# The shared expert's last 64 channels computed by token beside the router and carried in the expert rows

## The chip, the cores and the metric

The kernel runs on one NeuronCore of one Trainium2 chip. The time is that of one execution on the device in microseconds, as a median over runs. A core has five engines that matter here, each with its own queue of instructions: TensorE (PE in the profile; its weight loads are PEld), VectorE (DVE), ScalarE (ACT), GpSimd (POOL) and SyncE (SP), which here issues most of the DMA transfers.

## The reference

Everything is float32. 2048 tokens of 256 channels go through a layer norm, an attention-like block (convolution, gates, a scan over time, a perceptron), another norm and a residual, and then through a mixture of experts. The change is in the last part:

```python
shared = silu(x @ sw_gate) * (x @ sw_up) @ sw_down        # 704 inner channels
logits = x @ router_w.T                                   # 8 experts
top_w, top_i = top_k(softmax(logits), 2);  top_w /= sum(top_w)
h = silu(einsum('th,ehi->eti', x, w_gate)) * einsum('th,ehi->eti', x, w_up)   # 176 inner channels
expert_out = einsum('eti,eih->eth', h, w_down)
routed = einsum('eth,te->th', expert_out, combine)        # combine: the two weights, which sum to 1
out = routed + sigmoid(x @ shared_gate_w)[:, None] * shared
x = x + layernorm(out)
```

The shared expert has 704 = 5 x 128 + 64 inner channels, so in chunks of 128 there are five whole ones and a tail of 64. A routed expert has 176 = 128 + 48.

## The kernel before, in words

The tokens are worked in 8 blocks of 256 (`TB`), each seen as two halves of 128 (`NT`). A matrix product over 256 channels is two accumulating TensorE products (`product`, line 385), and each shows in the profile as two records.

*The three stages.* From 0 to about 360 us the attention, the perceptron, the routing and, for blocks 0 to 3, the shared expert are interleaved: every part of a block is a generator or a list of named steps, each step has a place (one unit is one of the perceptron's eight chunks), and all steps are sorted by place (`places`, `runs`). `runs` gives `route` of a block 8 places and `shared` nine evenly spaced ones (`evenly(NS + 4)`, with NS = 5). Within that order the compiler's scheduler may still move an instruction that is ready ahead of one that is not; each engine then executes its own list in order. `behind(...)` pins the order on the named engines where it is used. Then, from about 398 to 488 us, the routed experts are worked in 36 blocks of 128 rows (`in_turn`, `routed`), four steps deep: while block i is being transposed, i-1 does its gate and up products, i-2 its second transposes and i-3 its down product. At the end (`closing`, a list written out by hand) the shared expert of blocks 5 to 7 is interleaved with fetching, combining, normalizing and storing. Block 4's shared expert (`kept`) and the first three chunks of block 5's fill TensorE at the turn from the first stage to the second.

*`route(b)`* (lines 755 to 835). Normalizes the tokens into `ln` with `W` = 259 values to a row (256 channels, the first pair number, the chosen expert, the weight), transposes them to `yT` (channels on partitions), multiplies by `w_r` (9 columns: 8 logits and the shared gate), copies the logits to `lg` on VectorE, finds the two best, makes the weight and the gate on ScalarE (a tanh) and GpSimd, counts ranks with two small products, and scatters each token's row twice into the DRAM table `xs` by four indirect DMAs from GpSimd's queue, sorted by expert. `ln` has two buffers.

*`shared(b)`* (lines 840 to 877). For each of five chunks: gate and up products from `yT` into one PSUM bank, silu on ScalarE, product on VectorE into `shid`. Sixth step: one chunk that holds 64 up and 64 gate channels, so half as many products. Then for each half of the tokens a down product over six chunks of `shid` and `s_down`, of which the sixth is padded with zero rows, and the gate is applied by ScalarE (blocks 0 to 4) or VectorE (blocks 5 to 7, line 872).

*The turn.* `tables` works out from the counts where each expert's rows start and which expert each of the blocks of 128 rows belongs to; `fill` writes zero rows behind each expert's last one (eight DMAs on SP's queue, line 935). A branch (`tc.If`, for a few extra blocks) follows.

*`routed(i)`* (lines 937 to 986). SP reloads 128 rows into `xb` (4 buffers), after all scatters; TensorE transposes them, VectorE copies to `xT` and works out `pair` and `share` from the row's last three values; TensorE multiplies by the expert's gate and up weights (352 columns); silu and product go into one of two halves of `padded`, 256 wide with zeros behind the 176; two transposes, a copy on ScalarE (`hT`), and a down product of two steps, where the second has 48 weight rows and zeros. ScalarE scales by `share` (minus the weight for the first choice, one minus it for the second), and GpSimd's queue scatters the result into `ys`. VectorE's queue has `pair` of a block ahead of the copy to `xT` of an earlier one. `pair` has eight buffers, freed as the scatter of its block has ended.

*The closing.* `fetch` reads both rows of each token back (`g`), `combine` adds them (line 999 to 1002), `finish` normalizes and stores; `finish_last` does so for each half of block 7.

PSUM has eight banks: two "A", one "B", three "M", one "S", one "D". `route` takes "M", and so does the perceptron.

Of the kernel before, what the change touches and what calls it, by code (L numbers as in the profile page):

```python
# [9 lines left out]
F32 = mybir.dt.float32  # L10
# [9 lines left out]
P = 128  # L20
# [7 lines left out]
def kernel(ctx: ExitStack, tc: tile.TileContext, a: dict, out: bass.AP):  # L28
# [21 lines left out]
    assert T % TB == 0 and NT == 2 and KC == 2 and P < I <= 2 * P and TAIL == 64 and E == 8  # L50
# [34 lines left out]
    W = C + 3  # L85
    zeros = const.tile([P, W], F32, name="zeros")
    nc.gpsimd.memset(zeros, 0.0)
    nc.gpsimd.memset(zeros[:, C : C + 1], float(T * TOPK))
# [32 lines left out]
    def in_rows(ap):  # L121
        return ap.rearrange("(k p) n -> p k n", p=P)
# [82 lines left out]
    s_gu = wpool.tile([P, KC, (2 * NS + 1) * P], F32, name="s_gu")  # L205
# [7 lines left out]

    s_down = wpool.tile([P, NS + 1, C], F32, name="s_down")
    nc.sync.dma_start(s_down[:, 0:NS, :], in_rows(a["sw_down"][0 : NS * P, :]))
    nc.sync.dma_start(s_down[0:TAIL, NS, :], a["sw_down"][NS * P :, :])
# [4 lines left out]
    w_r = const.tile([P, KC, E + 1], F32, name="w_r")  # L221
# [69 lines left out]
    def tables_ready():  # L291

        to_columns((r_rows, w_r))
        nc.vector.tensor_copy(count, count_i)
        nc.vector.tensor_scalar(first_rows, experts_iota, float(ES), None, ALU.mult)
        nc.vector.tensor_scalar(block_rows, count, float(P), None, ALU.mult)
        nc.gpsimd.tensor_copy(first_pair, first_pair_i)
        nc.gpsimd.memset(seen, 0.0)
        nc.gpsimd.memset(s_down[TAIL:, NS, :], 0.0)
        nc.gpsimd.memset(shid[TAIL:, NS, :], 0.0)  # L300
# [91 lines left out]
    shid = act.tile([P, NS + 1, TB], F32, name="shid")  # L392
# [342 lines left out]
    KEEP_FROM, LATE_FROM, AHEAD, OFTEN = 4, 5, 3, 36  # L735
# [18 lines left out]
    def route(b):  # L754
# [5 lines left out]
        normalize("R", ln[:, :, 0:C], x_tiles[b], mv, rs)  # L760
        nc.gpsimd.tensor_copy(ln[:, :, C], first_pair[:, b * NT : (b + 1) * NT])
        yield
        yT = act.tile([P, KC, TB], F32, tag="yT", name=f"yT_{b}", bufs=NB - KEEP_FROM + 1)
        nc.scalar.copy(yT, to_channels("M", ln))
        yield
        po = psum("M")
        for n in range(NT):
            product(
                po[:, n * 16 : n * 16 + E + 1],
                [yT[:, k, tok(n)] for k in range(KC)], [w_r[:, k, :] for k in range(KC)],  # L770
            )
        lg = small.tile([P, NT, E + 1], F32, tag="lg", name=f"lg_{b}")
        nc.vector.tensor_copy(
            lg, po[:, 0 : NT * 16].rearrange("p (n e) -> p n e", n=NT)[:, :, 0 : E + 1]
        )
# [13 lines left out]
        nc.gpsimd.tensor_scalar(ln[:, :, C + 2], th[:, :, 0], 0.5, 0.5, ALU.mult, ALU.add)  # L789
        nc.gpsimd.tensor_scalar(gate, th[:, :, 1], 0.5, 0.5, ALU.mult, ALU.add)  # L790
        idf = small.tile([P, NT, TOPK], F32, tag="idf", name=f"idf_{b}")
        nc.vector.tensor_copy(idf, idx[:, :, 0:TOPK])
        nc.gpsimd.tensor_copy(ln[:, :, C + 1], idf[:, :, 0])
# [46 lines left out]
    def shared(b, banks=cycle("S"), shid=shid):  # L840

        t = live[b]
# [4 lines left out]
        for f in range(NS + 1):  # L847
            po = psum(next(banks))
            if f < NS:
                product(po[:, 0:TB], chunk(f), rhs)  # L850
                product(po[:, TB:], chunk(NS + f), rhs)
                nc.scalar.activation(shid[:, f, :], po[:, 0:TB], AF.Silu)
                nc.vector.tensor_tensor(shid[:, f, :], shid[:, f, :], po[:, TB:], ALU.mult)  # L853
            else:
                product(po[:, 0:TB], chunk(2 * NS), rhs)
                nc.scalar.activation(shid[0:TAIL, f, :], po[TAIL:, 0:TB], AF.Silu)
                nc.vector.tensor_tensor(  # L857
                    shid[0:TAIL, f, :], shid[0:TAIL, f, :], po[0:TAIL, 0:TB], ALU.mult
                )
            yield  # L860
        f_ = part_of[b] if b >= LATE_FROM else new_part(b)
        for n in range(NT):
            pn = psum(next(banks))[:, 0:C]
            product(
                pn, [shid[:, f, tok(n)] for f in range(NS + 1)],
                [s_down[:, f, :] for f in range(NS + 1)],
# [70 lines left out]
    def routed(i, row_i, off_i, of):  # L937
# [3 lines left out]
        xb = moe.tile([P, W], F32, tag="xb", name=f"xb_{i}", bufs=4)  # L941
        after(nc.sync.dma_start(xb, xs[bass.ds(at, P), :]).ins, scatters)
        pt = psum("A")
        for k in range(KC):
            nc.tensor.transpose(pt[:, tok(k)], xb[:, tok(k)], ident)  # L945
# [4 lines left out]
            pair, xb[:, C + 1 : C + 2], of[:, i : i + 1], xb[:, C : C + 1], ALU.not_equal, ALU.add  # L950
# [4 lines left out]
            share, xb[:, C + 1 : C + 2], of[:, i : i + 1], xb[:, C + 2 : C + 3], ALU.not_equal,  # L955
            ALU.subtract,
# [8 lines left out]
        h = padded[:, i % 2, :]  # L965
# [67 lines left out]
    def evenly(n):  # L1033
# [15 lines left out]
        (shared, NB, evenly(NS + 4)),  # L1049
# [47 lines left out]
    def keep():  # L1097
        nonlocal kept, shids
        more = wpool.tile([P, NS + 1, TB], F32, tag="w_gate", name="shid2")
        nc.gpsimd.memset(more[TAIL:, NS, :], 0.0)  # L1100
        shids = cycle((more, shid))
        kept = shared(KEEP_FROM, all_banks, next(shids))
        next(kept)
# [6 lines left out]
    for place, _, run in steps:  # L1110
        if place >= (NB + 2) * NF and not closed:
# [20 lines left out]
            )  # L1132
        run()
# [4 lines left out]
    padded = moe.tile([P, 2, C], F32, name="padded")  # L1138
    nc.gpsimd.memset(padded[:, :, I:], 0.0)
# [21 lines left out]
    for b in range(LATE_FROM, NB):  # L1161
# [10 lines left out]
        5.3 5.4 5.5 6.0 6.1 C5 C0 5.6 A0 5.7 C1  # L1172
        6.2 A5 N0 6.3 A1 6.4 X0 N5 C2 6.5 N1 C6 7.0 X5 A2 7.1 X1 C3 6.6 N2 A3 6.7 X2 A6 C4
        7.2 A4 N3 7.3 X3 N6 C7 7.4 N4 7.5 X6 X4 7.6 L0 7.7 L1
# [40 lines left out]
```

## Time and profile before

| | |
|---|---|
| median of 3 runs | 542.26 us (542.12 to 542.28) |
| the profiled execution | 542.94 us, its span 541.1 us |
| TensorE busy | 519.6 us, 96%, 2532 records |
| VectorE, ScalarE, GpSimd busy | 331.8, 218.4 and 165.0 us |
| granted TensorE clock | 0.993 |
| router products | 64 records of 128x9 |
| shared expert, gate and up | 352 records of 128x256 |
| shared expert, down | 192 records of 128x256 |
| reloads of rows | 36 of 129.5 KB |

A profile's line for an instruction gives its start in us from the span's start, its length in us, the engine, the line of the kernel, the operation, output and inputs, and behind "x" how many of them were merged. In brackets stands how long the engine had been idle before it and what ended that. A line for a stretch gives the stretch, its length, and the busy time of each engine with its number of instructions, then the granted clock, the DMA engines' share and the rate. Matmuls overlap one another, so that their lengths add up to more than the time they take; the distance from one group's start to the next one's is the pace. A line of the chain gives start, length and what the end of the kernel waited for then.

### The profile page before, as it was taken

How to read it: one execution, taken by the hardware profiler on the slowest of the kernel's cores; microseconds unless marked ns; L12 is line 12 of the kernel's file. 1: busy time of each engine (PE TensorE's matmuls, PEld its weight loads, DVE VectorE, ACT ScalarE, POOL GpSimd, SP SyncE). 2: the span in 40 equal slices, each digit the busy share in tenths (PEclk: the TensorE clock that was granted, in tenths of full speed). 3: DMA queues.
4: the chain of work that ended last, by engine and by line, in shares of the span. 5: the costliest groups of instructions: out<-in, count | busy, mean ns of one | idle time of the engine just before them, and what ended most of it. 6: DMA issues, size and time to landing. Idle time of an engine off the chain costs nothing. (4 is left out here: it accounts for less than half of the span.)

```text
span 541.1 us, 8015 instructions
## 1 busy us (share of the span) xinstructions
PE 519.6 (96%) x2532; PEld 433.8 (80%) x2532; DVE 331.8 (61%) x1100; ACT 218.4 (40%) x500; POOL 165.0 (30%) x297
## 2 busy tenths in 40 slices
PE   8999999999999999999999999998999999999992
PEld 5877677888888888888888888887867777777881
DVE  4788998896997987966824223232444444432883
ACT  4655554544644545433313313222124444442340
POOL 7233202203442432414105204023304334342351
PEclk9999999999999999999999999999999999999997
DMA  4981101001001110110000901001323333314621
GB/s 124 377 250 20 19 2 19 1 1 21 20 21 19 40 18 4 40 21 31 10 1 30 315 15 41 0 2 39 120 80 104 94 99 101 102 56 129 238 79 58
DMA packets 31344, 37.37 MB, mean 69 GB/s; under 512 B 4824, under 2 KB 26180, under 8 KB 31302
## 3 DMA queue, kind: packets, MB, share of 16 engines
q1 hardware_dynamic: 27440, 28.37, 18.6%
q0 software_dynamic: 3584, 8.48, 4.6%
q8 instruction: 21, 0.34, 0.3%
q14 instruction: 21, 0.17, 0.1%
q10 hardware_dynamic: 278, 0.01, 0.0%
HBM read 22.34 MB, written 13.18 MB: 66 GB/s over the span
## 5 line engine op out<-in xcount | busy, mean ns | idle before, releaser
L385 PE MATMUL psM<-h2T,w_gate 128*128 128x256 f32 x256 | 66.4, 381 | 0.0
L385 PE MATMUL psM<-h2T,w_val 128*128 128x256 f32 x256 | 66.1, 379 | 0.0
L710 PE MATMUL psD<-w_out,hid 128*128 128x256 f32 x256 | 63.5, 380 | 0.1
L982 POOL DMA_INDIRECT ys<-yb,pair x36 | 35.4, 983 | 70.6 <-ACT yb L981 59.4
L385 PEld LDWEIGHTS psM<-h2T,w_gate 128*128 128x128 f32 x256 | 47.8, 190 | 8.1 <-DVE o L631 1.3
L710 PEld LDWEIGHTS psD<-w_out,hid 128*128 128x128 f32 x256 | 48.4, 190 | 6.9 <-DVE hid L721 0.5
L385 PEld LDWEIGHTS psM<-h2T,w_val 128*128 128x128 f32 x256 | 48.6, 190 | 6.5
L385 PE MATMUL psM<-m_w,xT 128*128 x144 | 48.9, 462 | 0.7 <-DVE shid L853 0.4
L720 ACT ACTIVATE hid<-psM 128x256 f32<-128x256 f32 x64 | 24.1, 376 | 60.8 <-PE psM L385 60.7
L721 DVE TENSOR_TENSOR hid<-hid,psM 128x256 f32<-128x256 f32 x64 | 26.3, 411 | 31.3 <-ACT hid L720 31.0
L329 POOL TENSOR_SCALAR ln_rs<-ln_mv 128x2 f32<-128x2 f32 (+1 forms) x33 | 8.6, 261 | 117.3 <-DVE ln_mv L321 103.9
L828 POOL DMA_INDIRECT xs<-ln,rows x32 | 32.4, 1011 | 18.6 <-DVE rows L824 8.0
L385 PE MATMUL psA<-yT,s_gu 128*128 128x256 f32 x144 | 34.7, 383 | 2.7 <-DVE shid L853 2.7
L385 PE MATMUL psD<-m_w,hT 128*128 x144 | 37.2, 381 | 0.0
L949 DVE TENSOR_SCALAR pair<-xb,of 128x1 int32<-128x1 f32 x36 | 9.8, 272 | 42.1 <-DMA ys<-yb,pair 33.2
L385 PEld LDWEIGHTS psA<-yT,s_gu 128*128 128x128 f32 x144 | 26.7, 190 | 6.5 <-DVE shid L853 3.3
L385 PEld LDWEIGHTS psM<-m_w,xT 128*128 128x128 f32 x144 | 24.6, 191 | 8.9 <-DVE shid L853 0.6
L385 PEld LDWEIGHTS psD<-m_w,hT 128*128 128x128 f32 x144 | 24.6, 191 | 2.4 <-ACT yb L981 0.5
L330 POOL TENSOR_TENSOR ln_rs<-ln_rs,neg_half 128x2 f32<-128x2 f32 (+1 forms) x33 | 25.3, 766 | 2.2
L981 ACT ACTIVATE yb<-psD,share 128x256 f32<-128x256 f32 x36 | 17.0, 473 | 19.9 <-PE psD L385 16.8
L966 ACT ACTIVATE padded<-psM 128x176 f32<-128x176 f32 x36 | 11.4, 317 | 33.5 <-PE psM L385 27.2
L385 PE MATMUL psA<-s_down,shid 128*128 128x256 f32 x96 | 22.4, 381 | 0.7 <-DVE shid L857 0.7
(266 smaller groups left out, 1073.6 us busy)
## 6 DMA issues: line engine op xcount, KB each, us to landing
xb<-xs SPq DMA_DIRECT2D x36, 129.5 KB
g<-ys SPq DMA_DIRECT2D x8, 512.0 KB
xs<-zeros SPq DMA_DIRECT2D x16, 129.5 KB
x<-in_L_attn_x_dram SPq DMA_DIRECT2D x8, 256.0 KB
decay<-by_head SPq DMA_DIRECT2D x14, 128.0 KB
out_dram<-f SPq DMA_DIRECT2D x7, 256.0 KB
m_w<-in_L_ffn_w_gate_dram SPq DMA_DIRECT2D x2, 704.0 KB
m_w<-in_L_ffn_w_up_dram SPq DMA_DIRECT2D x2, 704.0 KB
```

Source lines behind the costliest of these rows:

```text
L329: nc.gpsimd.tensor_scalar(rs, mv[:, :, 1], EPS, None, ALU.add)
L330: nc.gpsimd.tensor_tensor(rs, rs, neg_half[:, 0:nt], ALU.pow)
L385: nc.tensor.matmul(po, lhs[i], rhs[i], start=(i == 0), stop=(i == len(lhs) - 1))
L710: nc.tensor.matmul(total[:, n * C : (n + 1) * C], hids[f][:, tok(n)], w_out[:, f, :], start=(f == 0 and n == 0), stop=(f == NF - 1 and n = ...
L720: nc.scalar.activation(hid, po[:, 0:TB], AF.Silu)
L721: nc.vector.tensor_tensor(hid, hid, po[:, TB:], ALU.mult)
L828: inst = nc.gpsimd.indirect_dma_start(out=xs, out_offset=bass.IndirectOffsetOnAxis(ap=rows[:, c : c + 1], axis=0), in_=ln[:, n, :], in_off ...
L949: nc.vector.tensor_scalar(pair, xb[:, C + 1 : C + 2], of[:, i : i + 1], xb[:, C : C + 1], ALU.not_equal, ALU.add)
L966: nc.scalar.activation(h[:, 0:I], po[:, 0:I], AF.Silu)
L981: nc.scalar.activation(yb, po[:, 0:C], AF.Copy, scale=share)
L982: inst = nc.gpsimd.indirect_dma_start(out=ys, out_offset=bass.IndirectOffsetOnAxis(ap=pair, axis=0), in_=yb, in_offset=None, bounds_check= ...
```

## The change

The shared expert's tail leaves `shared` and `shid`. Where the router multiplies a token's channels by 9 columns, it now multiplies by 137: 64 up, 64 gate, 8 logits and the gate (`w_r` moves behind them in `s_gu`). ScalarE and VectorE make silu(gate) times up by token (`end`), and GpSimd multiplies it by the shared gate into the token's row. A row of `xs` is now 3 numbers, 256 channels, 64 tail values and 16 zeros, W = 339 values. In `routed` the hidden values are written over the reloaded channels, so that the 176 hidden values, the 64 tail values and the zeros stand side by side, 256 wide, and the second transposes take all of them; `padded` goes, and `xb` has 6 buffers. The second down weights of every expert get the 64 tail rows of `sw_down` below their 48 (one more DMA, 64 rows to each of 8 experts). Each token has two rows and its two weights sum to one, so the tail is added once, and the gate is in it already. `evenly` gets one place fewer, the hand-written closing is arranged anew, and the memsets of the padding rows of `s_down` and `shid` go.

```diff
-    W = C + 3
+    X0 = 3
+    T0 = X0 + C
+    ROW, H0 = T0 + TAIL, T0 - I
+    W = H0 + 2 * P
...
-    s_gu = wpool.tile([P, KC, (2 * NS + 1) * P], F32, name="s_gu")
+    s_gu = wpool.tile([P, KC, (2 * NS + 1) * P + E + 1], F32, name="s_gu")
...
-    s_down = wpool.tile([P, NS + 1, C], F32, name="s_down")
-    nc.sync.dma_start(s_down[:, 0:NS, :], in_rows(a["sw_down"][0 : NS * P, :]))
-    nc.sync.dma_start(s_down[0:TAIL, NS, :], a["sw_down"][NS * P :, :])
+    s_down = wpool.tile([P, NS, C], F32, name="s_down")
+    nc.sync.dma_start(s_down, in_rows(a["sw_down"][0 : NS * P, :]))
...
-    w_r = const.tile([P, KC, E + 1], F32, name="w_r")
+    w_r = s_gu[:, :, (2 * NS + 1) * P :]
...
-        normalize("R", ln[:, :, 0:C], x_tiles[b], mv, rs)
-        nc.gpsimd.tensor_copy(ln[:, :, C], first_pair[:, b * NT : (b + 1) * NT])
+        normalize("R", ln[:, :, X0:T0], x_tiles[b], mv, rs)
+        nc.gpsimd.tensor_copy(ln[:, :, 0], first_pair[:, b * NT : (b + 1) * NT])
+        nc.gpsimd.memset(ln[:, :, ROW:], 0.0)
...
             product(
-                po[:, n * 16 : n * 16 + E + 1],
-                [yT[:, k, tok(n)] for k in range(KC)], [w_r[:, k, :] for k in range(KC)],
-            )
+                po[:, n * C : n * C + P + E + 1],
+                [yT[:, k, tok(n)] for k in range(KC)], [s_gu[:, k, 2 * NS * P :] for k in range(KC)],
+            )
+        by_token = po.rearrange("p (n e) -> p n e", n=NT)
...
+        nc.vector.tensor_copy(lg, by_token[:, :, P : P + E + 1])
+        end = small.tile([P, NT, TAIL], F32, tag="end", name=f"end_{b}", bufs=1)
+        nc.scalar.activation(end, by_token[:, :, TAIL:P], AF.Silu)
+        nc.vector.tensor_tensor(end, end, by_token[:, :, 0:TAIL], ALU.mult)
...
+        nc.gpsimd.tensor_tensor(
+            ln[:, :, T0:ROW], end, gate.unsqueeze(2).to_broadcast([P, NT, TAIL]), ALU.mult
+        )
...
-        for f in range(NS + 1):
+        for f in range(NS):
             po = psum(next(banks))
...
-            else:
-                product(po[:, 0:TB], chunk(2 * NS), rhs)
-                nc.scalar.activation(shid[0:TAIL, f, :], po[TAIL:, 0:TB], AF.Silu)
-                nc.vector.tensor_tensor(
-                    shid[0:TAIL, f, :], shid[0:TAIL, f, :], po[0:TAIL, 0:TB], ALU.mult
-                )
...
-                pn, [shid[:, f, tok(n)] for f in range(NS + 1)],
-                [s_down[:, f, :] for f in range(NS + 1)],
+                pn, [shid[:, f, tok(n)] for f in range(NS)], [s_down[:, f, :] for f in range(NS)],
...
-        xb = moe.tile([P, W], F32, tag="xb", name=f"xb_{i}", bufs=4)
+        xb = moe.tile([P, W], F32, tag="xb", name=f"xb_{i}", bufs=XB)
...
-            nc.tensor.transpose(pt[:, tok(k)], xb[:, tok(k)], ident)
+            nc.tensor.transpose(pt[:, tok(k)], xb[:, X0 + k * P : X0 + (k + 1) * P], ident)
...
-        h = padded[:, i % 2, :]
+        h = xb[:, H0:]
...
-        (shared, NB, evenly(NS + 4)),
+        (shared, NB, evenly(NS + 3)),
...
+            nc.sync.dma_start(
+                m_we[I - P : I - P + TAIL, :, KC * GU + C :],
+                a["sw_down"][NS * P :, :].unsqueeze(1).to_broadcast([TAIL, E, C]),
+            )
...
-        5.3 5.4 5.5 6.0 6.1 C5 C0 5.6 A0 5.7 C1
-        6.2 A5 N0 6.3 A1 6.4 X0 N5 C2 6.5 N1 C6 7.0 X5 A2 7.1 X1 C3 6.6 N2 A3 6.7 X2 A6 C4
-        7.2 A4 N3 7.3 X3 N6 C7 7.4 N4 7.5 X6 X4 7.6 L0 7.7 L1
+        5.3 5.4 6.0 C5 C0 5.5 A0 5.6 C1
+        6.1 A5 N0 6.2 A1 6.3 X0 N5 C2 6.4 N1 C6 7.0 X5 A2 6.5 X1 C3 7.1 N2 6.6 A3 X2 A6 C4
+        7.2 A4 N3 C7 7.3 X3 N6 7.4 N4 X6 7.5 X4 L0 7.6 L1
```

## The prediction

> **What bounds the kernel now.** I read the page's busy lines first, then the stretches of the span, then the costliest TensorE groups, then the order of time.
>
> ```profile
> PE 519.6 (96%) x2532; PEld 433.8 (80%) x2532; DVE 331.8 (61%) x1100; ACT 218.4 (40%) x500; POOL 165.0 (30%) x297
> ```
>
> TensorE is busy 96%, but its matmuls overlap (a 128x256 one lasts 380 ns), so busy is not yet pace. The pace is in the order of time:
>
> ```profile
> 298.50 1.89 PE L385 MATMUL psS<-yT,s_gu 128*128 128x256 f32 x8
> 300.22 1.03 PE L385 MATMUL psM<-h2T,w_gate 128*128 128x256 f32 x4
> ...
> 304.54 0.60 PE L376 MATMUL psM<-ident,ln 128*128 128x128 f32 x4
> 304.98 1.03 PE L385 MATMUL psA<-yT,s_gu 128*128 128x256 f32 x4
> 305.84 1.03 PE L385 MATMUL psM<-h2T,w_gate 128*128 128x256 f32 x4
> ...
> 308.87 0.96 PE L385 MATMUL psM<-w_r,yT 128*128 128x9 f32 x8
> 309.68 2.84 PE L385 MATMUL psS<-s_down,shid 128*128 128x256 f32 x12
> ```
>
> Eight 128x256 records from 298.50 to 300.22: 0.2155 us each. Four 128x128: 0.110 each. Eight 128x9: 0.101 each. (A product in the code is two records: the groups yT,s_gu have 144 + 80 + 64 + 32 + 32 = 352, which is 8 blocks x 22 products x 2.) Counting every form of each stretch with these paces fills 98 to 102% of nearly every 25 us between 100 and 360; TensorE has no holes there. The stretches:
>
> ```profile
> core 0: us, PE busy (x) PEld busy (x) DVE busy (x) ACT busy (x) POOL busy (x), PEclk, DMA share, GB/s
> 100.00:250.00 150.00, 149.93 (x758) 130.09 (x758) 124.69 (x417) 72.39 (x160) 45.84 (x86) 1.00 0.09 18
> 250.00:359.00 109.00, 107.85 (x529) 95.30 (x528) 41.53 (x159) 30.51 (x73) 26.22 (x43) 1.00 0.18 55
> 359.00:398.50 39.50, 37.55 (x184) 32.56 (x184) 15.72 (x71) 9.66 (x24) 11.80 (x16) 1.00 0.21 68
> 398.50:487.60 89.10, 88.38 (x423) 65.45 (x421) 39.03 (x139) 38.95 (x105) 32.44 (x33) 1.00 0.31 91
> 499.70:518.80 19.10, 19.10 (x90) 16.85 (x89) 16.32 (x43) 6.44 (x14) 6.97 (x17) 1.00 0.59 216
> 518.80:534.40 15.60, 11.48 (x52) 9.44 (x51) 11.58 (x30) 4.57 (x10) 6.88 (x15) 0.98 0.22 76
> ```
>
> TensorE sets the pace up to 487; VectorE has room from 250 to 488 (routing and shared stages), but is nearly as full as TensorE in the closing (16.32 of 19.10). The chain says so too: it is all PE to 518.80, then turns to VectorE and GpSimd, and TensorE itself waits there for the tail:
>
> ```profile
> 526.79 0.39 ACT shid L856
> 527.18 0.02 issue
> 527.21 0.41 DVE shid L857
> ```
>
> **The change part by part.** Sums are made against the profiled execution: 542.94 us, its span of 541.1 and 1.84 around it. The median, 542.26, is 0.68 lower, and that is taken off at the end.
>
> *Tail products.* Per block of 256 tokens, two products (gate/up chunk, two k) and one of six in each of two down products go: 4 products, 8 records, 8 x 0.2155 = 1.724 us of TensorE. Eight blocks: 64 records, 13.79 us.
>
> *Router made wider.* The same 64 records grow from 9 to 137 columns. Between 0.110 at 128 and 0.2155 at 256 columns, 137 cost 0.1174; 0.0164 more than now, 1.05 us in all. The weight loads stay as they are. Net TensorE: -12.74 us if nothing else bound.
>
> The page "TensorE: Matmul & The Clock Gate" of the Trainium skill (section "Back-to-back issue gap") gives 262 cycles for 256 columns, at 2.4 GHz 109 ns, and 134 cycles (56 ns) for 128; by it the removal would be worth an estimated 7.0 us, and the gain about half of mine. The rows above show 215 ns and 110 ns for these f32 records, so I go by the rows.
>
> *Up to 359 us.* Tails of blocks 0 to 2 (24 records, 5.17 us) lie here, where the pace is TensorE's alone; seven routers add 0.92. Net -4.25. Each route adds on VectorE one 128x128 product (between the 128x32 row, 188 ns, and the 128x176 one, 336: about 0.30 us) behind a ScalarE silu (between 205 and 317 ns: 0.28), on GpSimd a product by the gate (between 281 ns for 128x2 and 1342 for 128x512: 0.54) and a memset (0.12). VectorE stands in line: the top-two search and whatever of the attention is queued behind wait for that silu. In exchange, later, VectorE loses a 64x256 product (0.41) and ScalarE a silu (0.38) per block. Cover: VectorE idle 25 of 150 us, GpSimd 104. The router's bank of the three "M" ones is held perhaps 0.7 us longer. Bounds: nothing, to 0.2 us per route (1.4); I take 0.3.
>
> *GpSimd beside VectorE.* The 128x2 power took 0.71 at 519.05 and 1.13 at 515.84, while VectorE ran two-input 128x512 operations: here GpSimd was the one that lengthened. "SBUF — State Buffer", section "Who interferes with whom", says that a VectorE instruction with two SBUF inputs and a GpSimd one that reads SBUF exclude each other and the later one blocks; by it VectorE could lose up to an estimated 0.54 us per route, which its idle time still covers.
>
> *Start.* The zero rows are 1356 instead of 1036 bytes (8 x 40 KB more on SP's queue at 30 us, ahead of the decay transfers), one small weight load less. The waits named for the zero rows near there are 0.3 and 0.5 us; bounds 0 to 0.5, taken 0.1. The extra 512 KB of down weights go on SP's queue at some 300 us, where the next on it, the filling at 383, is far off: nothing; without that cover 1.7 us at the 315 GB/s of that slice.
>
> *Turn from shared to routed, 359 to 398.5.* Removed: blocks 3 and 4, 16 records, 3.45 us; one router adds 0.13. But a chain runs through: the last block's router ends at 378.04, the rows are known at 382.5, SP issues fillings from 383.45 to 390.9 and the first reload at 393.21, which lands at 395.19; the first expert transpose is at 398.47, 3.1 us later, because TensorE is still at shared work. There is also a hole of 1.5 us at 371.7. After the change the work between router and first transpose is kept chunks f2 to f4 (5.17), two downs (4.31), small ones (0.6) and three chunks of block 5 (5.17), 15.3 us, against a chain of about 17.1 us (378.04 to 395.19), +0.3 for silu and product, +0.2 for the larger transfer: TensorE waits some 2 us. The router itself ends about where it did (tail and 1.5 us hole less, the second down now ahead of it). So the first transpose comes about 3.0 us earlier (395.5 for 398.5). Bounds 1.5 (the chain 1.5 longer) to 3.8 (all removed work and the 0.45 hole at 392.8).
>
> *Routed blocks.* 36 at 2.49 us, all TensorE (two transposes 0.22, gate/up 1.19, 0.22, down 0.86): the tail rides in rows 48 to 111 of the second down product, which was there already. Same time, unless a wait comes in (rival 2).
>
> *Closing.* Blocks 5 to 7: 24 records, 5.17 us, and the 0.69 that TensorE waits for the tail at 526.98: 5.86 by TensorE. By VectorE: from 499.7 (the first fetch lands) it works some 27 of 34.6 us, loses two products (0.82), and so cannot end sooner than 6 us before now. Neither end is likely to be reached, since both would have to run full; the low bound is what VectorE and the last down lose by themselves, 0.82 + 0.43 + 0.69 = 1.9. I take 4.5, near TensorE's because TensorE leads up to 518.8. What then comes late is the combining and normalizing on VectorE.
>
> Sum: -4.25 + 0.3 + 0.1 - 3.0 - 4.5 = -11.35; 542.94 - 11.35 = 531.6, as a median 530.9. I say 531.0, the likeliest case.
>
> **Rivals.** (1) *The closing is VectorE's.* For it: the chain from 518.8 to 528.8 has no matmul in it, VectorE 85% full before. Against: that stretch is itself late because TensorE brings block 7's first chunk only at 518.6. Then 1.9 of 4.5 are left, perhaps with 1.5 less at the turn: 533.6 to 535.1; 534.3.
>
> (2) *The routed stage gets a wait; slower.* The hidden rows are now written into the reloaded rows' buffer, so a buffer is held until the second transposes, and its reload is released at 1.6 us into a block's period, not at 0.2; six buffers in place of four give back two periods, which the longer hold takes. A reload lands about 2.0 us after issue (393.21 to 395.19), perhaps 0.3 more now: some 4.0 us after the period's start, 1.5 into the next one. Ahead of each xT copy VectorE's queue has the pair number of a block three on, which reads that buffer:
>
> ```profile
> 440.50 0.38 PE L945 MATMUL psA<-ident,xb 128*128 128x128 f32 x2
> ...
> 443.21 1.35 PE L385 MATMUL psM<-m_w,xT 128*128 x4
> ```
> ```profile
> 441.63 0.27 DVE L949 TENSOR_SCALAR pair<-xb,of 128x1 int32<-128x1 f32 x1 [1.33 <-DMA ys<-yb,pair]
> 441.82 0.41 DVE L947 COPY xT<-psA 128x256 f32<-128x256 f32 x1
> ```
>
> It starts now at 1.13 into the period; at 1.5 the xT copy would end at 2.1, and TensorE needs it at 2.7. So 0.6 us of room: no stall. If the landing comes 0.6 + 0.34 later, 33 blocks lose 0.34 each and the gain is gone; 0.4 more, and it is 544. For: the room shrinks from 1.0. Against: transfers are at 31% of their engines.
>
> (3) *Route's longer bank and silu stall TensorE* between 100 and 360, where VectorE is 83% full: 0.6 us for each of seven routes, 4.2: 534.9.
>
> (4) *All of TensorE's saving shows*: -12.74 and both holes (0.69, 0.45): 529.1 profiled, 528.4 median.
>
> **How the numbers follow.** My forecast (529.5 to 533) 0.50; rival 4 below it 0.10; rivals 1 and 3 (533 to 537) 0.26; some of both, or a small stall of kind 2 (537 to 541) 0.06; rival 2 beyond no gain 0.07; a gain and a loss that cancel 0.01. 0.2% (1.1 us) is about what a measurement of this kernel can tell from no change. Faster 0.92, within 0.01, slower 0.07. The range from 528.4 (rival 4) to 536.5 leaves out some 0.04 below and 0.15 above.
>
> **What would show it.** Right: 2468 TensorE records in place of 2532, the 64 of the router at 137 columns at a pace near 0.117 us; the first expert transpose near 391.6 (398.5 - 4.25 + 0.4 - 3.0); the routed period still 2.49; end of the last product some 11 us earlier. Wrong: a routed period above 2.49 with pair waiting for the reload; TensorE waits for lg or end between 100 and 360; the closing's chain on VectorE from the first fetch on; a hole over 3 us before the first expert transpose.

## The result, and the profile after

| | before | changed |
|---|---|---|
| median, measured side by side | 542.19 us (541.77 to 542.28, 4 runs) | 534.98 us (534.43 to 536.48, 4 runs) |
| ratio | | 0.9873, 95% interval 0.9851 to 0.9895 |
| the profiled execution | 542.94 us, span 541.1 | 536.48 us, span 534.6 |

The changed kernel is faster by 7 us. The forecast was 531.0, with a range of 528.4 to 536.5: the sign and the range hold, and the time is 4.0 us above the likeliest case. The changed kernel's profiled execution is its slowest of four. It holds a stretch at half clock, described below; its mean granted clock was 0.986, that of the other three 0.988 to 0.991.

What was to go did go. On the page of the changed kernel TensorE has 2468 records instead of 2532 and is 8.8 us less busy; the row of the granted clock, in 40 slices of 13.4 us, has a 7 at the turn, where the kernel before has nines up to its last slice:

```profile
PE 510.8 (96%) x2468; PEld 423.1 (79%) x2468; DVE 332.5 (62%) x1100; ACT 216.8 (41%) x500; POOL 170.9 (32%) x309
...
PEclk9999999999999999999999999999979999999996
```

The stretches of the changed kernel, as before in the order stretch, length, busy time and instructions of each engine, clock, DMA share and rate:

```profile
core 0: us, PE busy (x) PEld busy (x) DVE busy (x) ACT busy (x) POOL busy (x), PEclk, DMA share, GB/s
...
250.00:352.70 102.70, 102.70 (x505) 90.77 (x504) 40.55 (x159) 29.74 (x73) 25.95 (x45) 1.00 0.24 68
352.70:390.70 38.00, 34.73 (x169) 29.55 (x168) 13.21 (x62) 9.14 (x23) 12.25 (x17) 1.00 0.26 81
390.70:400.10 9.40, 7.07 (x19) 4.26 (x20) 4.47 (x18) 1.09 (x4) 0.00 (x0) 0.64 0.29 83
400.10:484.00 83.90, 83.90 (x405) 62.72 (x403) 37.61 (x129) 37.91 (x102) 32.45 (x33) 1.00 0.37 108
...
495.00:513.00 18.00, 16.86 (x78) 14.55 (x77) 14.94 (x38) 5.11 (x12) 7.74 (x16) 1.00 0.65 241
513.00:528.00 15.00, 9.14 (x40) 7.05 (x38) 12.24 (x34) 5.17 (x11) 7.46 (x16) 0.94 0.24 84
```

TensorE has no hole from 250 us to the end of the perceptron and none in the routed stage. Between the two it loses 3.3 of 38 us, and then 2.3 of 9.4 us at a clock of 0.64. In the closing it is no longer full.

The same can be told by marks that both traces have: the end of the perceptron (the last sum into `h` of line 731, 729 before), the first scaling of an expert block (`yb`), the first fetch of the pairs' results (`g`), the last normalizing product (`f`), all by their starts in us.

| kernel (profiled execution) | perceptron's end | first `yb` | first `g` | last `f` | turn | routed | closing |
|---|---|---|---|---|---|---|---|
| before | 359.23 | 405.34 | 495.59 | 533.84 | 46.11 | 90.25 | 38.25 |
| changed | 353.12 | 402.51 | 491.60 | 527.32 | 49.39 | 89.09 | 35.72 |
| difference | -6.11 | | | | +3.28 | -1.16 | -2.53 |

The four differences add up to -6.52, that of the spans (-6.5). So the first stage gave more than was forecast (-3.85), the closing less (-4.5), and the turn, which was to give 3.0, took 3.3.

**The turn.** TensorE's order of time in the changed kernel has three holes there. In brackets is what ended each:

```profile
362.64 2.97 PE L387 MATMUL psA<-yT,s_gu 128*128 128x256 f32 x13
367.40 2.43 PE L387 MATMUL psA<-s_down,shid 128*128 128x256 f32 x10 [1.79 <-DVE shid L863]
...
372.26 1.10 PE L387 MATMUL psM<-s_gu,yT 128*128 128x137 f32 x8
```
```profile
383.62 1.89 PE L387 MATMUL psS<-yT,s_gu 128*128 128x256 f32 x8
387.00 1.97 PE L387 MATMUL psM<-yT,s_gu 128*128 128x256 f32 x8 [1.49 <-DVEq L1157]
388.80 1.89 PE L387 MATMUL psA<-yT,s_gu 128*128 128x256 f32 x8
390.66 0.41 PE L948 MATMUL psA<-ident,xb 128*128 128x128 f32 x2
393.24 0.69 PE L948 MATMUL psA<-ident,xb 128*128 128x128 f32 x2 [2.17 <-DVE xT L950]
394.08 2.69 PE L387 MATMUL psM<-m_w,xT 128*128 x4 [0.16 <-DMA xb<-xs]
```

(The eight 137-column records of the router, at 372.26, take 0.93 us to the next group at 373.19: 0.116 each, where 0.1174 was forecast.)

The last line is the first gate and up products of the expert blocks. In the kernel before they were:

```profile
399.70 1.42 PE L385 MATMUL psM<-m_w,xT 128*128 x4 [0.36 <-DVE shid L853]
```

*First hole, 1.79 us.* The down products wait for block 3's last product in `shid`, that for its silu, and the silus stand in ScalarE's queue behind the layer norm of the last block. That norm waits for GpSimd's power, which stands behind a scatter of block 6. ScalarE first, then GpSimd:

```profile
364.87 1.09 ACT L341 ACTIVATE ln<-x,ln_nb,ln_rs 128x256 f32<-128x256 f32 x2 [5.75 <-DVE ln_nb L339]
365.87 0.36 ACT L862 ACTIVATE shid<-psS 128x256 f32<-128x256 f32 x1
366.13 0.37 ACT L862 ACTIVATE shid<-psM 128x256 f32<-128x256 f32 x1
366.39 0.65 ACT L862 ACTIVATE shid<-psA 128x256 f32<-128x256 f32 x2
```
```profile
362.60 0.96 POOL L838 DMA_INDIRECT xs<-ln,rows  x1 [0.30 <-issue]
...
363.92 0.72 POOL L332 TENSOR_TENSOR ln_rs<-ln_rs,neg_half 128x2 f32<-128x2 f32 x1
```

The silus of four chunks stood behind the norm, though ScalarE had been idle for 5.75 us ahead of it.

*Second hole, 1.49 us.* At the branch (line 1157). In the kernel before all three chunks of block 5 came behind the branch; now the first is ahead of it, and VectorE reaches the branch only after that chunk's product, at 385.96.

*Third hole, 2.17 us.* The second transposes wait until the first `xT` copy is done. VectorE's queue has `pair` and `share` of the second and third block ahead of that copy, and each `pair` waits until its reload has landed:

```profile
390.55 0.27 DVE L952 TENSOR_SCALAR pair<-xb,of 128x1 int32<-128x1 f32 x1 [4.16 <-DMA xb<-xs]
...
391.62 0.27 DVE L952 TENSOR_SCALAR pair<-xb,of 128x1 int32<-128x1 f32 x1 [0.29 <-DMA xb<-xs]
...
392.39 0.27 DVE L952 TENSOR_SCALAR pair<-xb,of 128x1 int32<-128x1 f32 x1 [0.32 <-DMA xb<-xs]
...
392.76 0.41 DVE L950 COPY xT<-psA 128x256 f32<-128x256 f32 x1
```

The transposes of 390.66 were done by 391.07, and the copy came at 392.76.

*Half clock.* Then the first gate and up products ran at half speed, as the granted clock of three stretches of 3.41 us shows (same columns as above):

```profile
389.53:392.94 3.41, 1.54 (x8) 0.88 (x6) 1.79 (x8) 0.38 (x1) 0.00 (x0) 1.00 0.73 203
392.94:396.36 3.42, 2.97 (x6) 1.70 (x7) 2.00 (x8) 0.00 (x0) 0.00 (x0) 0.50 0.32 93
396.36:399.77 3.41, 3.41 (x10) 2.10 (x9) 0.67 (x2) 0.51 (x2) 0.00 (x0) 0.50 0.00 0
```

From the first gate and up products to the first `yb` took 8.43 us here (394.08 to 402.51) and 5.64 before (399.70 to 405.34), so that the 6.8 us at half the clock cost this execution 2.8 us.

**The closing.** The chain of the changed kernel leaves TensorE with the first fetch, and from there it runs through VectorE, GpSimd and ScalarE (start, length, engine and what). These are some of its pieces; TensorE has one more in it, 0.71 us at 520.97:

```profile
491.75 0.30 ACT shid L862
492.05 4.87 DMA g<-ys
496.94 0.70 DVE f L1002
...
498.75 0.66 DVE ln_st L322 x2
500.02 0.65 POOL ln_nb L1012
500.67 1.24 POOL ln_rs L332
502.24 0.48 issue
502.72 0.59 ACT f L1016
```

In the kernel before the chain was TensorE's up to 518.80.

### The profile page after: what moved, and what is told of

Read it like the earlier page. It is cut to its first block, busy times and chain, and to the rows that moved or that the text cites. A ratio compares the mean times of both kernels' runs of the same rounds, so it can differ in the third digit from the quotient of the medians.

```text
span 534.6 us, 7921 instructions
## 1 busy us (share of the span) xinstructions
PE 510.8 (96%) x2468; PEld 423.1 (79%) x2468; DVE 332.5 (62%) x1100; ACT 216.8 (41%) x500; POOL 170.9 (32%) x309
## 5 line engine op out<-in xcount | busy, mean ns | idle before, releaser
L387 PE MATMUL psM<-m_w,xT 128*128 x144 | 51.1, 479 | 0.2 <-DMA xb<-xs 0.2
L387 PEld LDWEIGHTS psM<-m_w,xT 128*128 128x128 f32 x144 | 25.7, 198 | 8.8 <-issue 1.5
L387 PE MATMUL psA<-yT,s_gu 128*128 128x256 f32 x128 | 30.4, 383 | 0.0
L950 DVE COPY xT<-psA 128x256 f32<-128x256 f32 x36 | 15.2, 423 | 19.5 <-PE psA L948 19.3
L952 DVE TENSOR_SCALAR pair<-xb,of 128x1 int32<-128x1 f32 x36 | 9.8, 273 | 27.7 <-DMA xb<-xs 27.7
L969 ACT ACTIVATE xb<-psM 128x176 f32<-128x176 f32 x36 | 11.4, 317 | 38.0 <-PE psM L387 37.1
L387 PEld LDWEIGHTS psA<-yT,s_gu 128*128 128x128 f32 x128 | 23.7, 190 | 3.0
```

What stands on the lines that cost most here:

```text
L387: nc.tensor.matmul(po, lhs[i], rhs[i], start=(i == 0), stop=(i == len(lhs) - 1))
L950: nc.vector.tensor_copy(xT, pt[:, 0 : KC * P].rearrange("p (k t) -> p k t", k=KC))
L969: nc.scalar.activation(h[:, 0:I], po[:, 0:I], AF.Silu)
```

## The experiments

The medians of the kernel before beside these runs were 541.3 to 541.6 us; beside the changed kernel it was 542.19. So a difference from the changed kernel's 534.98 may be off by 0.6 to 0.9 us, and the ratio to the kernel before of the same round (0.9873 for the changed kernel) is given where it matters. Unless another kernel is named, the edits are made in the changed kernel.

**1. Is it the clock?** Between block 5's chunks and the first expert transposes, two unused pairs of products (eight records of 256 columns, 1.72 us) keep TensorE busy; their result goes nowhere.

```diff
+    po = psum("S")
+    with behind(PE):
+        for _ in range(2):
+            product(
+                po[:, 0:TB], [s_gu[:, k, 0:P] for k in range(KC)],
+                [live[LATE_FROM]["yT"][:, k, :] for k in range(KC)],
+            )
```

> The changed kernel with two products more (8 records of 128x256, 1.72 us) that nobody uses, in TensorE's queue between the three chunks ahead and the first expert transpose; nothing is taken away. My theory of the turn: TensorE waits 2.2 us there for the first copy of xT, and the granted clock then is at half for some 6.8 us; the wait itself stays, but with the products in it the clock stays full, and the first blocks run at 2.49 us: 2.0 to 3.0 us less than the changed kernel's 535.0, so 532 to 533. Rival: the wait was the whole loss and the low clock lay under it: no change, or up to 1.7 us more (535 to 536.7).

Measured: 534.90 us (534.40 to 536.09), ratio 0.9888: the 532 to 533 did not come, and the rival's "no change" did. In its profiled execution, 534.46 us, the clock is 1.00 from 390 to 402 us, and from the first gate and up products to the first `yb` took 5.94 us instead of 8.43; but these products started 0.97 us later, counted from the perceptron's end. Only this one of its executions was traced (the mean clocks of the four are 0.988 to 0.994), so how much of the median the clock has isn't settled by it. Filling the wait with work that nobody uses wins nothing.

**2. Useful work in the holes.** Four and five of block 5's chunks ahead of the expert blocks instead of three, each taken out of the closing.

```diff
-    KEEP_FROM, LATE_FROM, AHEAD, OFTEN, XB = 4, 5, 3, 36, 6
+    KEEP_FROM, LATE_FROM, AHEAD, OFTEN, XB = 4, 5, 5, 36, 6
...
-        5.3 5.4 6.0 C5 C0 5.5 A0 5.6 C1
+        6.0 C5 C0 5.5 A0 5.6 C1
```

> The changed kernel with four chunks of block 5 in place of three ahead of the routed blocks, and one entry fewer in the closing. The same 8 records in the same place, but of use. Theory of the turn: as with the unused products, 532 to 533, and 1.72 us of TensorE's work less in the closing. If TensorE sets the closing's pace, that comes on top (530.5 to 531.5); if VectorE and GpSimd do, nothing more comes (532 to 533).

> The changed kernel with all five chunks of block 5 ahead of the routed blocks and two entries fewer in the closing: 3.45 us of TensorE's work moved from the end to the turn. The hole there is about 3 us, so it is filled. If TensorE sets the closing's pace: 529 to 530.5. If the fetch and then VectorE set it: the routed stage ends no earlier than with four (the fifth chunk pushes it back by up to 1 us), 532 to 533.5.

Measured: 535.32 us (533.82 to 536.23) with four and 534.08 (533.79 to 534.80) with five (ratios 0.9880 and 0.9869); both lie above all that was expected of them. With five, 3.45 us of TensorE work had left the closing (two chunks, by the pace of 0.2155), and the closing of its trace lasted 35.60 us where the changed kernel's lasted 35.72. TensorE's work does not set its length.

**3. The removal alone.** The kernel before, with the tail left out and not computed anywhere, `evenly` and the closing as in the change.

```diff
-        for f in range(NS + 1):
+        for f in range(NS):
...
-        (shared, NB, evenly(NS + 4)),
+        (shared, NB, evenly(NS + 3)),
```

> The kernel before without the 64-channel tail: its chunk, its sixth product in the downs and the freed places go as in the change, and the closing's order is the change's, but nothing is put in its place (router 9 columns, rows of 1036 bytes, xb of 4 buffers, padded kept); the output lacks the tail. This is the removal alone. If the loss against my forecast is the turn's and the closing's own (less work on TensorE, the same chains), it comes out only a little below the changed kernel: 533 to 534.5, and its trace shows a hole and a low clock at the turn too. If what the change adds (wider rows, wider router, the work by token) had eaten the gain, it comes out near my forecast, 529 to 531.

Measured: 534.62 us (534.35 to 535.27), a little above the 533 to 534.5 expected; ratio 0.9874 beside 0.9873 for the whole change. Without any of the additions it is no faster within what these runs can tell, and has the same holes: 1.8 us for `shid`, 1.5 at the branch, 1.9 for `xT`. So what is added costs little in total, and the shortfall comes with the removal. Its turn lasted 48.12 us in the trace, 2.0 more than before with 3.45 us of work less.

**4. What sets the closing.** The sum of the residual (one 128x512 VectorE operation per block) left out for blocks 0 to 6, in the changed kernel and in the kernel before; the output is then without the residual.

```diff
-        nc.vector.tensor_tensor(f_, f_, x_tiles[b], ALU.add)
```

> The changed kernel without the residual sum of blocks 0 to 6 in the closing: seven VectorE operations of 128x512 at 0.68 us, 4.7 us in all (the output lacks that sum). If after the change VectorE with GpSimd behind the fetch sets the closing, as its chain says: 2.0 to 4.0 us less, 531 to 533 for 535.0. If TensorE still sets it: no change, 534.5 to 535.5.

> The same edit in the kernel before (the output lacks that sum). By my prediction TensorE led its closing up to 518.8 us and only the last part was VectorE's: the chain holds 1.8 us of these sums, so 1.0 to 2.0 us less than 541.5, about half of what the same edit gives after. If VectorE set the whole closing already before the change, the two savings are alike (2 to 4 us).

Measured: changed 533.69 us (532.23 to 534.42), before 540.31 (539.27 to 541.64). The medians give 1.3 each (by the ratios, 0.9860 and 0.9978, 0.7 and 1.2): less than the 2 to 4 us expected of the changed kernel, and they don't tell the two kernels apart. In the traces the closing fell from 35.72 to 33.58 in the changed kernel (-2.1) and from 38.25 to 37.03 in the kernel before (-1.2). Why the medians show less of it is open. Beside experiment 2 the traces still say which work counts: some 4.2 us of VectorE's (seven sums at a pace of 0.60) taken away shorten the changed closing by 2.1, 3.45 us of TensorE's by 0.1.

**5. The first hole.** The last block's third layer norm is placed later and, on ScalarE, behind the four silus.

```diff
-    last_route = (1.4, 2.0, 5.6, 6.6, 6.7, 7.9, 7.9, 7.9)
+    last_route = (1.4, 4.6, 5.6, 6.6, 6.7, 7.9, 7.9, 7.9)
...
+    def late_step(run):
+        with behind(ACT):
+            next(run, None)
```

(`late_step` runs that one step.)

> The changed kernel with one order of ScalarE's changed: the last block's normalizing before its router stands behind the four silus that were queued after it, not ahead of them. It waits there for GpSimd, which has four scatters of the block before in its queue, and the silus wait with it; TensorE stands for 1.8 us. If that hole delays the chain router, ranks, scatters, filling, reload: everything behind comes 1.3 to 1.8 us earlier, 533.2 to 533.7. If the chain hangs on GpSimd alone: 534.5 to 535.2.

Measured: 533.24 us (532.23 to 533.51), 1.7 less than the changed kernel (1.7 by the ratio too, 0.9841, whose interval of 0.9814 to 0.9868 overlaps the changed kernel's). TensorE's line in its trace:

```profile
365.61 2.43 PE L387 MATMUL psA<-s_down,shid 128*128 128x256 f32 x10 [0.28 <-DVE shid L863]
```

The hole shrank from 1.79 to 0.28, and the later norm made nothing late: the router's products follow at 370.47, where they were at 372.26. Counted from the perceptron's end they come 1.5 us earlier, and the first gate and up products 1.4.

**6. The third hole.** `pair` and `share` on VectorE behind their own block's `xT` copy, in every expert block.

```diff
-        nc.vector.tensor_copy(xT, pt[:, 0 : KC * P].rearrange("p (k t) -> p k t", k=KC))
-        pair = small.tile([P, 1], I32, tag="pair", name=f"pair_{i}", bufs=8)
...
+        copied = nc.vector.tensor_copy(xT, pt[:, 0 : KC * P].rearrange("p (k t) -> p k t", k=KC)).ins
+        with tc.issue_after(copied):
+            pair = small.tile([P, 1], I32, tag="pair", name=f"pair_{i}", bufs=8)
```

(`share` likewise.)

> The changed kernel with each block's pair and share on VectorE placed behind the same block's copy of xT. At the turn the pair numbers of blocks 1 and 2 stood ahead of the first copy and waited for their reloads, so that the copy came at 392.8 where its transposes were done at 391.1. If VectorE's order makes that hole: first copy near 391.3, the hole 0.7 in place of 2.2 us, 1.0 to 1.5 us less (533.5 to 534). If only the chain of reloads counts (block 1's rows land at 391.6, block 2's at 392.4): 0 to 0.5 less. The routed period stays 2.49 us by my reckoning; if pair was in the way there, it falls.

Measured: 531.89 us (531.42 to 532.19), 3.1 less than the changed kernel (2.8 by the ratio, 0.9822) and about twice what was expected. TensorE's order of time in its trace:

```profile
390.03 0.41 PE L948 MATMUL psA<-ident,xb 128*128 128x128 f32 x2
391.10 0.41 PE L948 MATMUL psA<-ident,xb 128*128 128x128 f32 x2 [0.66 <-DMA xb<-xs]
392.06 1.42 PE L387 MATMUL psM<-m_w,xT 128*128 x4 [0.55 <-DMA xb<-xs]
```

The first gate and up products start at 392.06 instead of 394.08, at a clock of 1.00, and only reloads are waited for. Of the 2.0 us, 0.5 was there at the perceptron's end; 1.5 come from the order, as expected. The rest fits the half clock's absence: from these products to the first `yb` took 5.65 us here, 8.43 in the changed kernel's trace and 7.2 to 7.6 in four others that have the third hole (experiments 3, 4, 5 and 9). The mean clocks of all four executions point the same way, 0.992 to 0.993 against 0.986 to 0.991, but they don't say where the half clock lay.

**7. The same order in the kernel before.**

> The kernel before, with VectorE's pair and share behind the block's own xT copy, the edit that won 3.1 us in the changed kernel. Theory: VectorE's order costs something only where the third and fourth reload land after the first transposes; in the kernel before all four had landed by 398.1 us, the first xT copy was at 398.89 us: 541.0 to 542.2 us, no difference. Rival: the order costs the same in both kernels, and the changed one only shares it: 538.5 to 539.5 us.

Measured: 540.74 us (540.02 to 541.20) beside 541.33, ratio 0.9981 (0.9968 to 0.9993). The order costs 0.6 us there (0.3 up to the first gate and up products of the trace) and 3.1 in the changed kernel (1.5). So it isn't a property of the stage: it bites where the second and third reload land behind the first transposes, and in the kernel before shared work filled TensorE until they had landed.

**8. Both moves, and the branch.** Experiments 5 and 6 in one kernel; then the same with the cycle of PSUM banks turned on by one, which puts the first of block 5's chunks behind the branch again.

```diff
+    next(all_banks)
     late = {b: shared(b, all_banks, next(shids)) for b in range(LATE_FROM, NB)}
```

> The changed kernel with both moves together: VectorE's two products per expert block (pair and share) behind that block's own xT copy, and the last block's third layer norm on ScalarE behind the four silus of the shared expert. Alone they gave 531.89 and 533.24 us against 534.98. If the two holes stand one after the other on TensorE's path (the hole before the down products at 367 us, the wait for xT at 391 us), the gains add: 530.1 to 530.6 us. If the start of the expert blocks is set by the reloads of the pairs' rows, which come when the fillings have landed, the time won at 367 us is partly lost again in front of the first transpose: 531.2 to 531.9 us.

> As the run with both moves, and the cycle of PSUM banks turned on by one before block 5's chunks, which puts the first of these chunks behind the branch on the expert blocks' number instead of ahead of it; VectorE then comes to the branch without that chunk's product. The wait of 1.49 us at the branch should go from the trace. Theory: it hides nothing but a wait for the reloads (the first landed at 390.55 us in the changed kernel, at the end of the third chunk), so that 0 to 0.4 us are won. Rival: the branch's wait stands on the path, and 1.2 to 1.5 us are won against the run with both moves.

Measured: both moves 530.13 us (530.05 to 530.33), ratio to the kernel before 0.9793 (0.9774 to 0.9811), the fastest here. 4.85 us less than the changed kernel, and 3.1 + 1.7 = 4.8: the two add (by the ratios 4.3, and 2.8 + 1.7 = 4.5). With the banks turned on 530.89 us (530.30 to 532.51), no gain. TensorE with both moves, and then with the banks turned on as well:

```profile
384.85 1.97 PE L387 MATMUL psM<-yT,s_gu 128*128 128x256 f32 x8 [1.48 <-DVEq L1165]
...
388.70 0.41 PE L948 MATMUL psA<-ident,xb 128*128 128x128 f32 x2 [0.16 <-DMA xb<-xs]
389.89 0.41 PE L948 MATMUL psA<-ident,xb 128*128 128x128 f32 x2 [0.77 <-DMA xb<-xs]
390.75 1.42 PE L387 MATMUL psM<-m_w,xT 128*128 x4 [0.45 <-DMA xb<-xs]
```
```profile
382.68 1.99 PE L387 MATMUL psM<-yT,s_gu 128*128 128x256 f32 x8 [1.01 <-ACTq L1166]
...
388.97 0.44 PE L948 MATMUL psA<-ident,xb 128*128 128x128 f32 x2 [0.84 <-DMA xb<-xs]
390.01 0.41 PE L948 MATMUL psA<-ident,xb 128*128 128x128 f32 x2 [0.60 <-DVE xT L950]
390.96 1.42 PE L387 MATMUL psM<-m_w,xT 128*128 x4 [0.54 <-DVE xT L950]
```

The waits are 2.86 us in the one and 2.99 in the other, only in other places, and the gate and up products start within 0.2 us of each other. The wait at the branch, which was to go, shrank to 1.01, and ScalarE was now the late one. The hole at the branch was cover: once it shrinks, the wait for the reloads grows. The chain of the kernel with both moves says what sets the start of the expert blocks, the landing of the last filling and then the first reload, both from SP's queue:

```profile
382.54 3.30 DMA xs<-zeros
...
386.16 2.41 DMA xb<-xs
```

With the banks turned on that filling took 3.75 us, and the reload was issued 0.47 later. That the branch would be worth nothing even without any wait follows from this chain and was not run.

**9. The forecast's slower rival.** Four buffers for the reloaded rows instead of six.

```diff
-    KEEP_FROM, LATE_FROM, AHEAD, OFTEN, XB = 4, 5, 3, 36, 6
+    KEEP_FROM, LATE_FROM, AHEAD, OFTEN, XB = 4, 5, 3, 36, 4
```

> The changed kernel with four buffers for the pairs' rows instead of six, as the kernel before had; a buffer is now held until the second silu product and the down product have read it, so a reload is issued about two periods of 2.49 us later than with six. Theory (the reloads have slack in the routed stage: VectorE's pair waits for them, but TensorE does not): 534.5 to 535.8 us. The forecast's second rival with fewer buffers: the reload is on the path, each period grows by 0.1 to 0.5 us, 36 of them: 538 to 553 us.

Measured: 535.65 us (535.08 to 535.80), 0.7 more than the changed kernel (1.0 by the ratio, 0.9891). VectorE in the routed stage, with six buffers and then with four:

```profile
441.38 0.27 DVE L952 TENSOR_SCALAR pair<-xb,of 128x1 int32<-128x1 f32 x1 [0.76 <-DMA xb<-xs]
```
```profile
440.21 0.27 DVE L952 TENSOR_SCALAR pair<-xb,of 128x1 int32<-128x1 f32 x1 [0.89 <-DMA xb<-xs]
```

`pair` waits for the reload in nearly every block in either case (27.7 us in 34 times with six, 34.4 in 35 with four), and the period, once the first blocks are through, stays 2.49 us but for two blocks (2.95 and 2.54). TensorE has its `xT` in time all the same.

## Why the prediction was right, and where it was wrong

**Up to 359 us: forecast -3.85, in the traces -6.11.** The removal was sized by TensorE's pace alone, -5.17, with the words that TensorE "has no holes there". It had one, of 1.15 us, and the row for 250 to 359 us showed it: 107.85 busy of 109.00.

```profile
252.57 1.78 PE L385 MATMUL psA<-yT,s_gu 128*128 128x256 f32 x7 [1.15 <-DVE shid L853]
```

It waited for `shid` and went with the tail. Experiment 3 gives the removal by itself: from 55 us to the perceptron's end it wins 6.44, which is 5.17 + 1.15 and 0.1. The change wins 5.50 there, so all the additions cost 0.94 in these traces, where the forecast had 0.92 + 0.3 + 0.1; in eight of the nine other traces with the additions they cost 0.4 to 0.5. The remaining 0.6 of the 6.11 was there by 55 us, ahead of the first changed step of work; the kernel of experiment 7 has it as well, so it belongs to the one execution of the kernel before that was profiled. The pace of the router's records (0.116 for 0.1174) was right. Rival 3 fell: TensorE waits neither for `lg` nor for `end`.

**The turn: forecast -3.0, in the traces +3.28. This step failed.** It went by one chain, that of the reloads, and foresaw a wait of some 2 us and the first transposes near 391.6. They came at 390.66, but only because the first stage had given more: from the perceptron's end to them it was 37.54 us for 39.24, 1.7 of the 3.0. From there the forecast went straight into the expert blocks, where the trace has 5.0 us more up to the first `yb` (11.85 for 6.87). Three things were not in it:

- the last block's norm ahead of four silus on ScalarE (1.79 us; experiment 5 wins 1.7). In the kernel before the corresponding hole was 1.5 us, and the forecast counted it as gone with the tail.
- `pair` of the second and third block ahead of the first `xT` copy (2.17 us; experiment 6 wins 3.1). That order was described ahead of the prediction, and rival 2 weighed it for the steady period only. At the start of the stage the reloads land one after the other at 390.55, 391.62 and 392.39, and the queue makes the first block wait for the third.
- the half clock that followed in the profiled execution (2.8 us).

With both moves the turn lasts 43.92 us instead of 46.11: -2.2, within the bounds of 1.5 to 3.8. The saving that the step claimed existed; the order of two queues held it back. Of the 6.3 us between forecast and trace, the two orders are 2.7 (the first gate and up products of experiment 8 come that much earlier after the perceptron's end), the half clock is 2.8, and 0.8 is what the step promised too much.

**Routed blocks: forecast nothing, right.** The period is 2.49 us in both. The -1.16 in the table is mostly chance: the same stage took 88.45 and 89.48 us in two other traces without the change (experiments 4 and 7) and 90.09 with the removal alone (experiment 3), 88.45 to 89.45 in those with the change. Rival 2's mechanism is there in the form that was described, `pair` waiting for the reload by 0.5 to 0.9 us in most periods and by 1.86 in one, but its price was rightly put as nothing as long as `xT` is in time.

**The closing: forecast -4.5, in the traces -2.53.** The term was placed near TensorE's end of its bounds (1.9 to 5.86) "because TensorE leads up to 518.8". With 24 records less it was no longer first, and the chain of combining and normalizing took over from the fetch on, one of the signs of being wrong that the prediction had named. This was rival 1, and its value of 1.9 was nearer. In eight other traces of the changed kernel and its variants with all sums, the closing lasted 35.52 to 35.95 us, whatever happened at the turn.

**The sum.** Against the profiled executions -11.35 was forecast and -6.46 came, of which the first stage is +2.3 better, the turn 6.3 worse, the closing 2.0 worse and the routed stage 1.2 better. That the time stayed inside the range is partly luck: two stages gave 3.4 us more than forecast, one of them mostly by chance, and covered about half of the turn's miss. Rivals 1 and 3 stood at 534.3 and 534.9, and the time fell there: the first has its mechanism in the closing, and its 1.5 less at the turn is a part of the largest miss, without its cause; the third is coincidence.

## What to carry to other kernels

When work is taken from an engine that covers a hand-over between two stages, list for each other engine's queue what stands ahead of the first instruction that the next stage needs, because an order that cost little under the cover (0.6 us here) can then cost more than the hand-over was to win (3.1 us, the clock's share included, for 3.0). Where the bound of a term lies between two engines, take the busy time of the second one with the first one's savings already made; if both are near full, the gain may be near the smaller end, as here (2.5 between 1.9 and 5.86). A hole that a shorter wait would close is worth testing by itself: the one at the branch looked as good as the two others, and shrinking it by 0.5 us was worth nothing.

## What the runs showed of the hardware that was not expected

The granted clock fell to half after holes that were short. In the changed kernel's profiled execution TensorE was idle for 1.49 us before 387.00 and for 2.17 us before 393.24, and the clock was low for 6.83 us from 392.94 on. The variants with the third hole (experiments 3, 4, 5 and 9) and the one with four chunks ahead had 3.41 us of it there; the other variants had none.

The clock records of the traces show what this hangs on. From the first clock record of a trace on, the clock changed only after whole multiples of 3.413 us, in all 14 traces: in the changed kernel's, after 385.71 (113 of them) at full, 6.83 (2) at half and 126.29 (37) at full. So the traces can be cut into windows of that length, and the three stretches under "Half clock" are such windows. The kernel with both moves, with 1.48 us at the branch and waits of 0.16, 0.77 and 0.45 after it, has these at the same place:

```profile
388.39:391.80 3.41, 2.03 (x9) 1.17 (x9) 1.91 (x7) 0.38 (x1) 0.00 (x0) 1.00 0.77 206
391.80:395.22 3.42, 3.42 (x18) 2.32 (x17) 2.07 (x8) 0.96 (x3) 0.00 (x0) 1.00 0.21 59
```

The 14 traces have 2126 windows at full clock. In 18 of them TensorE was busy for 1.25 us or less, and half clock followed on every one (many lie at the kernel's end); in 11 it was busy for 1.49 to 1.80 us, and half clock followed on 3; in all others it was busy for 1.84 us or more, and on none did it follow. Half clock stayed after a window of 2.97 us of work and ended after those of 3.18 and more. So it was not the length of one hole that counted, but how much TensorE did in a window: between 1.25 and 1.84 us of 3.41 lies the limit. The first record begins 4.2 to 7.2 us after the span's start, differently in each execution, so that equal holes can end differently. With the unused products (waits of 0.53 and 1.42 us) the window had 2.19 us of work and the clock stayed; with four chunks ahead (0.49 and 1.32) it had 1.59, and half clock followed. This is read off the traces; no run moved a hole against the windows.

The Trainium skill, "TensorE: Matmul & The Clock Gate", section "What's actually happening", says that the clock goes to half after at least one idle window of about 3.4 us, and that these windows run freely. Length and free running agree with these traces. Idle throughout the window need not be: the one before 392.94 had 1.54 us of work, and half clock followed.

The GpSimd power of a 128x2 tile took 0.71 us at 503.10 and 1.26 at 500.64 in the changed closing, the longer one while VectorE added two 128x512 tiles. Three such lengthened powers stand in the changed kernel's closing (1.26, 1.13, 1.13), two in that of the kernel before (1.13, 1.12), and without the residual sums (experiment 4) there are three as well (1.26, 1.25, 1.25), so the work taken off VectorE did not make them fewer.
